# Two attention layers on one core: the last half block of the first layer turned on TensorE, and two sets of first scores placed anew

## The chip, the cores and the metric

The kernel runs on one core of a Trainium2 chip. Its time is the device time of one execution in microseconds, the median of several runs; the profile is of one execution of the same program. Five engines take part, each with its own instruction queue: TensorE (PE, with its weight loads PEld), VectorE (DVE), ScalarE (ACT), GpSimd (POOL) and SyncE (SP). DMAs are issued here from SP and POOL. Each queue runs in order: an instruction that waits holds up all that stand behind it on its engine.

## The reference

Two attention layers on an image batch x of shape 4 x 64 x 64 x 256, that is 4 images of N = 4096 tokens with C = 256 channels, in fp32.

```python
# layer 0
q, k, v = x @ Wq + bq, x @ Wk + bk, x @ Wv + bv          # 32, 32, 256 channels
attn = softmax(einsum('bnd,bmd->bnm', q, k))
x1 = gamma * einsum('bnm,bmc->bnc', attn, v) + x
# layer 1
f, g, v = x1 @ Wf + bf, x1 @ Wg + bg, x1 @ Wh + bh        # 32, 32, 128 channels
beta = softmax(einsum('bqd,bkd->bqk', g, f))
out = x1 + (einsum('bqk,bkd->bqd', beta, v) @ Wo + bo)
```

Layer 1 of an image needs the whole of layer 0 of that image: its keys and values come from every token of x1.

## The kernel before, in words

**Steps.** For each image b and layer l the queries are worked off in blocks j, and for each block all keys in steps i. Layer 0 has 16 blocks of 256 queries with 8 steps of 512 keys; layer 1 has 8 blocks of 512 queries with 16 steps of 256 keys. That is 128 steps a layer and 1024 in all, numbered n. In a step TensorE makes the scores (keys by queries, `Step.scores`, L595) into PSUM, ACT takes their exponential p (L611), and TensorE multiplies p by the values into an accumulator (L655 in layer 0, L673 in layer 1).

**Exact products in parts.** Where a step is split, p is cut into a high part (a second exponential on ACT, L605), a low part (DVE, L625) and a correction d (DVE, L630), and so are the values; TensorE then makes three sets of faster products, called "h", "l" and "d". All steps of layer 0 are split, and the even steps of layer 1; the odd steps of layer 1 take p whole. DVE also adds up the p of layer 1 for the softmax's denominator (p_sum, L644); some p are added by DMA instead (p_sum_moved, issued by POOL, L618 and L620). The p of these steps keep their SBUF buffer until that DMA has landed.

**PSUM.** Eight banks: the tag "st" holds one set of scores (two banks), "pair" two banks, which in layer 0 are the accumulators of the second half of the queries and in layer 1 a second buffer for scores, "acc0" and "acc1" one bank each, and "side" two buffers of one bank for everything else. In layer 1 the scores alternate between "st" and "pair"; in layer 0 all scores use "st", the first of each image too. The scores of step n + 2 are issued in step n.

**Projections between the steps.** While a step runs, small stages are put at given places: `put(n, slot, ...)` hangs a stage on step n, at "a" (before the step's cuts) or at "b" (after the scores of step n + 2). `plan` hangs them, at the first step of each block, by strings such as "2b 5a 5b": step offset and slot. A half block of 256 tokens goes through the stages load, turn (transposed to channels by tokens, xT), cut and rest (xT in a high and a low part, xh and xl), five stages for queries and keys (multiply into psqk, L439; take; add; cut; rest, which stores the result to qk_dram, L469), and three for the values (multiply into psv, L490; take; rest). The keys of both half blocks of 512 tokens are then loaded from qk_dram by four DMAs that POOL issues (L529), as soon as both are stored.

**How a half block is turned.** Only the 16 half blocks of image 0 in layer 0 are transposed by TensorE: natural tiles x_nat and an identity into a side bank, and ACT copies that to xT (L400, L401). All others are read from DRAM in 32 x 32 squares by eight DMAs (`load_squares`, L287), and DVE transposes inside the squares (L403). For layer 1 they are squares of x1_dram, which the end of each layer 0 block stores.

**The end of a layer 0 block.** `end_first` adds the accumulator halves (o, L693) and puts `residual(0)` and `residual(1)`, one for each 128 queries: x_new = o times gamma over the sum, plus x, on DVE (L701, L702, L704), a store to x1_dram on SP (L708), and an accumulating DMA to the output on POOL (L709). For all blocks but the last they hang on steps 1 and 2 of the next block; for the last on steps 0 and 1 of layer 1.

**The last half block.** Block 15 of layer 0 ends where layer 1 begins. Its half block, h = 15, is planned at the first step of layer 1 (`put_half(n, b, NH - 1, ...)`), with its load in step 2, its turn in step 5 and its projection in step 7. The keys of block 7, of which it is half, are used first by the scores of step 14, which are issued in step 12. In the same block the half block 15 of the next image is loaded (offset 9) and turned on DVE (offset 11).

**Order.** From step 8 on the order of instructions is the order in which the program writes them (`manual_schedule`); each engine's queue is that order. In a layer 1 step it is: stages of slot "a"; the cuts on DVE; the scores of step n + 2; stages of slot "b"; the sums that are due; the products "h" and "l" or the whole ones of this step; the "d" of the step before.

**Buffers that matter.** "small" has four buffers of 128 x 256 (x_res, x_new, y), "sums" one of 128 x 512 (the folded p_sum of a layer 1 block, idle in most of layer 0), "squares" two (squares, xh, xl and reloaded xT in turn).

Of the kernel before, what the change touches and what calls it, by code (L numbers as in the profile page):

```python
# [50 lines left out]
F32 = mybir.dt.float32  # L51
# [6 lines left out]
P = 128  # L58
QB = 512
# [188 lines left out]
def fast_path(ctx: ExitStack, tc: tile.TileContext, x, w0, w1, wo, bo, gamma, out, off):  # L248
# [46 lines left out]
            load_squares((b, 0, h), x[b, h * QB0 : (h + 1) * QB0, :])  # L295


    x_nat = {}
    LEAD_BUFS = sum(split[1])
    LEAD = V1 // NS  # L300

    def load_first(h):
        if h < NH:
            x_nat[h] = []
            for n in range(h * NS, (h + 1) * NS):
                x_nat[h].append(data.tile([P, C], F32, tag="v1", bufs=V1, name=f"x_nat_{n}"))
                nc.sync.dma_start(x_nat[h][-1], x[0, n * P : (n + 1) * P, :])

    for h in range(LEAD):
        load_first(h)  # L310


    ident = work.tile([P, NT, QB0], F32, tag="moved", bufs=1, name="ident")[:, 0, :P]
    make_identity(nc, ident)
    ones = const.tile([P, 1], F32, name="ones")
    nc.vector.memset(ones, 1.0)

# [31 lines left out]
    def side_psum(name):  # L349
        return ps_side.tile([P, QB], F32, tag="side", name=name)  # L350
# [38 lines left out]
    def transpose_stages(b, l, h):  # L389
        key = (b, l, h)  # L390
        lead = b == l == 0 and h % 2 == 1

        def turn():
            tag = "v1_parts" if lead else "xT"
            xT[key] = data.tile([P, NCC, QB0], F32, tag=tag, bufs=LEAD_BUFS if lead else 1, name=f"xT_{b}_{l}_{h}")
            if b == l == 0:
                ps = side_psum(f"psx_{h}").rearrange("p (c n) -> p c n", c=NCC)
                for c in range(NCC):
                    for t in range(NS):
                        nc.tensor.transpose(ps[:, c, t * P : (t + 1) * P], x_nat[h][t][:, c * P : (c + 1) * P], ident)  # L400
                nc.scalar.copy(xT[key], ps)  # L401
            else:
                nc.vector.transpose(  # L403
                    xT[key].rearrange("p c n -> p (c n)"), turned[key].rearrange("p c n -> p (c n)")
                )

        def cut():
            x_parts[key] = [
                (data if lead else work).tile(
                    [P, NCC, QB0],  # L410
                    F32R,
                    tag="v1_parts" if lead else "squares",
                    bufs=LEAD_BUFS if lead else 2,
                    name=f"x{what}_{b}_{l}_{h}",
                )
                for what in "hl"
            ]
            nc.scalar.copy(x_parts[key][0], xT[key])

        def rest():  # L420
            nc.vector.tensor_sub(x_parts[key][1], xT[key], x_parts[key][0].bitcast(F32))
            if b == l == 0:
                load_first(h + LEAD)

        return turn, cut, rest
# [149 lines left out]
    class Step:  # L575
# [10 lines left out]
        def scores(self):  # L586
            b, l, j, i = self.b, self.l, self.j, self.i
            n = 2 * QB // G[l]
            q0 = j * n % QB
            index = j * NI[1] + i  # L590
            tag = "pair" if l == 1 and index > 0 and index % 2 == 0 else "st"
            st = ps_main.tile([P, G[l], n], F32, tag=tag, name=f"st_{self.key}")
            for g in range(G[l]):
                kt = G[l] * i + g
                nc.tensor.matmul(  # L595
                    st[:, g, :],
                    k_t[b, l, kt // NT][:, kt % NT * P : (kt % NT + 1) * P],
                    q_t[b, l, j * n // QB][:, q0 : q0 + n],
                    start=True,
                    stop=True,  # L600
                )
            s_flat = st.rearrange("p g n -> p (g n)").rearrange("p (a n) -> p a n", n=QB0)
            if self.split:
                self.high = wide(f"high_{self.key}", self.n + 0.6, F32R)
                nc.scalar.activation(self.high, s_flat, AF.Exp, bias=down)  # L605
            kept = self.n - 0.3 if l == 0 else self.n + 1.8
            if l == 1 and i in self.moved:
                moved_until[0] = max(moved_until[0], self.n - 0.4) + 2.3
                kept = max(kept, moved_until[0])
            self.p = wide(f"p_{self.key}", kept)  # L610
            nc.scalar.activation(self.p, s_flat, AF.Exp)  # L611
# [77 lines left out]
    def end_first(b, j, acc, o, n_next):  # L689

        key = f"{b}_{j}"
        for s in range(NS):
            nc.vector.tensor_add(o[s], o[s], acc[2 * s + 1][:, :W])  # L693
        jj, part = divmod(j, QB // QB0)
        x_old = x_res.pop((b, j))

        def residual(s):
            def issue():
                n = (b * N + j * QB0) // P + s
                g = work.tile([P, 1], F32, tag="g", name=f"g_{key}_{s}")  # L700
                nc.vector.reciprocal(inverse[:, 0, n : n + 1], o[s][:, C : C + 1])  # L701
                nc.vector.tensor_mul(g, inverse[:, 0, n : n + 1], gamma_sb)  # L702
                x_new = small(f"x1_{key}_{s}")
                nc.vector.scalar_tensor_tensor(x_new, o[s][:, :C], g, x_old[s], ALU.mult, ALU.add)  # L704
                if part == 0 and s == 0:
                    x1_dram[b, jj] = dram.tile([QB, C], F32, name=f"x1_dram_{b}_{jj}")
                row = part * QB0 + s * P
                nc.sync.dma_start(x1_dram[b, jj][row : row + P, :], x_new)  # L708
                nc.gpsimd.dma_start(out_rows(b, j, s), x_new, accum_op=ALU.add)  # L709

            return issue

        n_next += j < NQ[0] - 1
        put(n_next, "b", residual(0))
        put(n_next + 1, "b", residual(1))

    def take_first_two(b, j, acc):

# [79 lines left out]

    def put_half(n, b, h, at):
        (turn, cut, rest), qk, v = project_stages(b, 1, h)  # L800
        load = lambda: load_squares((b, 1, h), x1_rows(b, h))
        put_all(n, at, (load, turn, cut, rest, qk[0], qk[1], qk[2], qk[3], qk[4], v[0], v[1], v[2]))

    def put_next(n, b, h, at):
# [10 lines left out]
    def put_values(m, b, h):  # L815
# [8 lines left out]
        put(m + 1, "a", v[1])  # L824
        put(m + 1, "b", v[2])

    def plan(n, b, l, j):
        if l == 0 and j >= 1:
            put_half(n, b, j - 1, "3b 5b 5b 6b 7b 8a 8b 8b 9b 8b 9a 11b")
            if b + 1 < B:  # L830
                put_next(n, b + 1, j - 1, "0b 1b 1b 2b 3b 4a 4b 4b 5b")
        if l == 1:
            if j == 0:
                put_half(n, b, NH - 1, "2b 5a 5b 6a 7b 8a 8b 8b 9a 8b 9a 9b")
            if b + 1 < B:
                if j == 0:
                    put_next(n, b + 1, NH - 1, "9b 11a 11b 12a 13b 14a 14b 14b 15b")
                else:
                    first, at = VALUES_AT[j]
                    for k, m in enumerate(at):  # L840
                        put_values(n + m, b + 1, first + k)
# [41 lines left out]
    for n, s in enumerate(steps):  # L883
# [50 lines left out]
        if l == 1:  # L934
            if s.last:
                o = take_first_two(b, j, acc)
            later.scores()
            run(todo.pop((n, "b"), []))

            while later_sums and (later_sums[0][1] <= n or vector_clock + later_sums[0][0] <= tensor_clock + AHEAD_OF):  # L940
                took, _, issue, _ = later_sums.pop(0)
                issue()
                vector_clock += took
            behind = steps[n - 1] if not s.first and steps[n - 1].split else None
            if s.last and behind:
                behind.products_second(acc, ("d",))
            s.products_second(acc, ("h", "l") if s.split else ("whole",))
            if not s.last and behind:
                behind.products_second(acc, ("d",))
            if s.last:  # L950
                vector_clock += 0.8
                end_second(b, j, acc, p_sum, o, n + 1)
        else:

            for half, what in ((0, "h"), (0, "l"), (1, "h"), (1, "l")) if s.first or s.last else ((0, "h"), (1, "h"), (0, "l"), (1, "l")):
                s.products_first(acc, half, what)
                if s.last and what == "l":
                    take_first(b, j, acc, o, half)
            if early:
                run([u for x in early for u in x[1] + x[2]])  # L960
            later.scores()
            run(todo.pop((n, "b"), []))
            for half in (0, 1):
                s.products_first(acc, half, "d")
            if s.last:
                end_first(b, j, acc, o, n + 1)
# [65 lines left out]
```

## Time and profile before

| | |
|---|---|
| Median of 3 runs | 3156.79 us (3154.54 to 3158.68) |
| Profiled execution, its own time | 3157.77 us |
| Its span, first to last instruction | 3155.9 us |
| Granted TensorE clock over the span | 0.995 |
| Instructions | 55119 |
| Steady layer 0, 100 to 515 us | PE busy 415.00 us, DVE 374.87, ACT 291.86 |
| First block of layer 1, image 0, 526 to 575 us | PE busy 43.88 of 49.00 us, DVE 42.05, ACT 32.90; clock 0.97 |
| Rest of layer 1, image 0, 575 to 830 us | PE busy 254.68 of 255.00 us, DVE 227.98, ACT 184.99 |

Rows of the groups view give for each kind of instruction its count and the mean time of one. Those that the change touches:

| Instruction | Count | Mean ns |
|---|---|---|
| transpose on TensorE, psx (L400) | 64 | 273 (median), pipelined |
| copy of it by ACT (L401) | 16 | 577 |
| transpose in squares on DVE (L403) | 112 | 708 |
| low and d cuts on DVE (L625, L630) | 534 and 527 under their first names | 1222, 1220 |
| x_new on DVE (L704) | 128 | 485 |
| store of x1 on SP, to landing (L708) | 128 | 1.7 us |
| square load from x1 on SP, to landing (L287) | 512 | 1.9 us |

A line of the timeline reads: start in us, length of the merged row, engine, source line, operation, what is written and read, how many instructions, and in brackets the engine's idle time before it and who ended that. PE rows are pipelined: the start of one row to the start of the next is the time that the engine gave to it. Idle time of DVE, ACT or POOL costs nothing by itself.

### The profile page before, as it was taken

To read this page: it belongs to the slowest core of one execution; us is meant where nothing else is said; L and a number is where in the kernel's file an instruction comes from. 1 tells how busy PE (TensorE), PEld (TensorE's weight loads), DVE (VectorE), ACT (ScalarE), POOL (GpSimd) and SP (SyncE) were. 2 spreads that over 40 slices of the span, in tenths; PEclk is the share of its full clock that TensorE was granted. 3 is DMA by queue.
4 is the path that set the end of the run, shared out by engine and by line. 5 is a ranking of instruction groups with operands and counts; after the bars stand their busy time and mean duration, and the time that the engine had idled before them with its cause. 6 is when DMAs were issued, how large, how long until landed. Compare 5 with 4: busy or idle time off the path is not lost. (4 is left out here: it accounts for less than half of the span.)

```text
span 3155.9 us, 55119 instructions
## 1 busy us (share of the span) xinstructions
PE 3099.8 (98%) x20036; PEld 2696.1 (85%) x20036; DVE 2755.2 (87%) x3360; ACT 2203.1 (70%) x2899; POOL 773.2 (24%) x1137
## 2 busy tenths in 40 slices
PE   8999999999999999999999999999999999999998
PEld 7999998666799999766679999976668999996665
DVE  7899889888888899898889998988887888888897
ACT  7677777677667677677766777767776666667775
POOL 4111113222411111322241111132234111132322
PEclk9999999999999999999999999999999999999999
DMA  4344445556644444656554444465565333335655
GB/s 123 75 93 85 90 88 122 121 115 121 121 84 89 87 93 84 131 117 118 118 107 93 84 92 84 94 129 114 118 123 99 65 65 73 63 82 113 116 107 94
DMA packets 446746, 314.55 MB, mean 100 GB/s; under 512 B 272802, under 2 KB 394404, under 8 KB 446468
## 3 DMA queue, kind: packets, MB, share of 16 engines
q0 software_dynamic: 109392, 184.43, 32.8%
q1 hardware_dynamic: 336164, 126.19, 16.9%
q8 instruction: 162, 2.65, 0.3%
q14 instruction: 116, 0.95, 0.1%
q10 hardware_dynamic: 912, 0.33, 0.0%
HBM read 128.71 MB, written 96.47 MB: 71 GB/s over the span
## 5 line engine op out<-in xcount | busy, mean ns | idle before, releaser
L605 ACT ACTIVATE high<-st,down 128x1024 fp32r<-128x1024 f32 x645 | 721.0, 1118 | 696.1 <-PE st L595 605.2
L611 ACT ACTIVATE p<-st 128x1024 f32<-128x1024 f32 x1024 | 1026.5, 1019 | 17.2 <-DMA p_sum_moved<-p 9.7
L625 DVE TENSOR_TENSOR low<-p,high 128x1024 fp32r<-128x1024 f32 x534 | 652.7, 1222 | 123.8 <-ACT p L611 119.4
L595 PE MATMUL st<-q,k 128*128 128x256 f32 (+1 forms) x3072 | 663.4, 324 | 13.3 <-DMA k<-qk_dram 7.4
L630 DVE SCALAR_TENSOR_TENSOR d<-low,high 128x1024 fp32r<-128x1024 f32 x527 | 643.0, 1220 | 15.6 <-PE acc L673 0.7
L595 PEld LDWEIGHTS st<-q,k 128*128 128x128 f32 x3072 | 473.4, 189 | 73.4 <-issue 16.4
L673 PE MATMUL acc<-p,v 128*128 128x512 f32 x1024 | 488.8, 600 | 1.1 <-DVE o L744 1.1
L655 PE MATMUL acc<-v0d,d 128*128 128x258 f32 x2048 | 336.1, 286 | 2.1 <-DVE d L630 2.0
L655 PE MATMUL acc<-v0h,high 128*128 128x258 f32 x2048 | 330.9, 284 | 1.2 <-ACT high L605 1.2
L655 PE MATMUL acc_pair<-v0l,low 128*128 128x256 f32 (+1 forms) x2048 | 329.9, 283 | 0.0
L655 PE MATMUL acc_pair<-v0h,high 128*128 128x258 f32 x2048 | 329.7, 283 | 0.0
L655 PE MATMUL acc_pair<-v0d,d 128*128 128x258 f32 x2048 | 328.8, 282 | 0.0
L655 PE MATMUL acc<-v0l,low 128*128 128x256 f32 (+1 forms) x2048 | 328.0, 282 | 0.6 <-DVE low L625 0.5
L709 POOL DMA_DIRECT2D out<-x x128 | 114.4, 894 | 837.0 <-DVE x L704 828.9
L644 DVE TENSOR_TENSOR p_sum<-p_sum,p 128x1024 f32<-128x1024 f32 x257 | 313.0, 1218 | 0.3
L673 PEld LDWEIGHTS acc<-p,v 128*128 128x128 f32 x1024 | 188.4, 191 | 144.2 <-issue 123.6
L655 PEld LDWEIGHTS acc<-v0d,d 128*128 128x128 f32 x2048 | 281.0, 189 | 3.8 <-DVE d L630 3.7
L655 PEld LDWEIGHTS acc<-v0h,high 128*128 128x128 f32 x2048 | 281.5, 189 | 3.0 <-issue 1.4
L655 PEld LDWEIGHTS acc<-v0l,low 128*128 128x128 f32 x2048 | 280.9, 189 | 1.8 <-DVE low L625 1.6
L655 PEld LDWEIGHTS acc_pair<-v0l,low 128*128 128x128 f32 x2048 | 282.3, 189 | 0.1
L655 PEld LDWEIGHTS acc_pair<-v0h,high 128*128 128x128 f32 x2048 | 281.9, 189 | 0.2 <-DVE o L693 0.2
L655 PEld LDWEIGHTS acc_pair<-v0d,d 128*128 128x128 f32 x2048 | 281.6, 189 | 0.0
(157 smaller groups left out, 4281.6 us busy)
## 6 DMA issues: line engine op xcount, KB each, us to landing
p_sum_moved<-p POOLq DMA_DIRECT2D x191, 512.0 KB, 4.8
x_res<-in_x SPq DMA_DIRECT2D x128, 128.0 KB, 3.1
qk_dram<-qk_parts SPq DMA_DIRECT2D x128, 128.0 KB, 2.1
x_res<-bias POOLq DMA_DIRECT2D x128, 128.0 KB, 4.0
out<-bias SPq DMA_DIRECT2D x128, 128.0 KB, 4.2
x_dram<-x SPq DMA_DIRECT2D x128, 128.0 KB, 1.7
out<-x POOLq DMA_DIRECT2D x128, 128.0 KB, 3.1
squares<-x_dram SPq DMA_DIRECT2D x512, 32.0 KB, 1.9
```

What stands on the lines that cost most here:

```text
L595: nc.tensor.matmul(st[:, g, :], k_t[b, l, kt // NT][:, kt % NT * P : (kt % NT + 1) * P], q_t[b, l, j * n // QB][:, q0 : q0 + n], start=Tru ...
L605: nc.scalar.activation(self.high, s_flat, AF.Exp, bias=down)
L611: nc.scalar.activation(self.p, s_flat, AF.Exp)
L625: nc.vector.tensor_sub(self.low, self.p, self.high.bitcast(F32))
L630: nc.vector.scalar_tensor_tensor(self.d, self.low.bitcast(F32), -UP, self.high.bitcast(F32), ALU.mult, ALU.add)
L644: nc.vector.tensor_add(p_sum, other, self.p)
L655: nc.tensor.matmul(acc[2 * s + which][:, :width], p[:, g, s * P : (s + 1) * P], v0[self.i][v][:, g, :width], start=self.first and what != ...
L673: nc.tensor.matmul(acc[which], v_part[:, g, :], p[:, g * NS : (g + 1) * NS, :], start=first and g == 0, stop=last and g == G[1] - 1,)
L709: nc.gpsimd.dma_start(out_rows(b, j, s), x_new, accum_op=ALU.add)
```

## The change

The x_new tiles of block 15 stay in SBUF and are transposed by TensorE into a side bank with an identity; ACT copies the bank to xT. They are not stored to x1_dram any more, and their half block isn't loaded in squares. The identity is written to DRAM once at the start, and each image loads it at block 8 of layer 0 into the "sums" buffer, since the SBUF place where it was made is reused. The residual of block 15 is hung on step 0 of layer 1, its first part at "a". The stages of the last half block move up: turn from offset 5 to 3, projection from 7 to 5. The first scores of layer 0 of images 1 to 3 use "pair" in place of "st". In the first step of layer 1 the products "h" and "l" come ahead of the scores of step 2.

```diff
-    x_nat = {}
+    rows = {}
...
+            rows[0, 0, h] = (tiles, ident)
...
     make_identity(nc, ident)
+    ident_dram = dram.tile([P, P], F32, name="ident_dram")
+    nc.sync.dma_start(ident_dram, ident)
...
-            if b == l == 0:
-                ps = side_psum(f"psx_{h}").rearrange("p (c n) -> p c n", c=NCC)
+            if key in rows:
+                tiles, unit = rows.pop(key)
+                ps = side_psum(f"psx_{b}_{l}_{h}").rearrange("p (c n) -> p c n", c=NCC)
                 for c in range(NCC):
                     for t in range(NS):
-                        nc.tensor.transpose(ps[:, c, t * P : (t + 1) * P], x_nat[h][t][:, c * P : (c + 1) * P], ident)
+                        nc.tensor.transpose(ps[:, c, t * P : (t + 1) * P], tiles[t][:, c * P : (c + 1) * P], unit)
                 nc.scalar.copy(xT[key], ps)
...
-            tag = "pair" if l == 1 and index > 0 and index % 2 == 0 else "st"
+            in_pair = index > 0 and index % 2 == 0 if l == 1 else b > 0 and j == i == 0
+            tag = "pair" if in_pair else "st"
...
                 x_new = small(f"x1_{key}_{s}")
+                if j == NQ[0] - 1:
+                    if s == 0:
+                        rows[b, 1, NH - 1] = ([], idents.pop(b))
+                    rows[b, 1, NH - 1][0].append(x_new)
...
-                nc.sync.dma_start(x1_dram[b, jj][row : row + P, :], x_new)
+                if j < NQ[0] - 1:
+                    nc.sync.dma_start(x1_dram[b, jj][row : row + P, :], x_new)
...
-        n_next += j < NQ[0] - 1
-        put(n_next, "b", residual(0))
-        put(n_next + 1, "b", residual(1))
+        if j < NQ[0] - 1:
+            put(n_next + 1, "b", residual(0))
+            put(n_next + 2, "b", residual(1))
+        else:
+            put(n_next, "a", residual(0))
+            put(n_next, "b", residual(1))
...
-        load = lambda: load_squares((b, 1, h), x1_rows(b, h))
+        load = nothing if h == NH - 1 else lambda: load_squares((b, 1, h), x1_rows(b, h))
...
+    def load_ident(b):
+        idents[b] = work.tile([P, QB], F32, tag="sums", bufs=1, name=f"ident_{b}")[:, :P]
+        nc.sync.dma_start(idents[b], ident_dram)
...
+        if l == 0 and j == NQ[0] // 2:
+            put(n, "b", lambda: load_ident(b))
...
-                put_half(n, b, NH - 1, "2b 5a 5b 6a 7b 8a 8b 8b 9a 8b 9a 9b")
+                put_half(n, b, NH - 1, "2b 3a 3b 4a 5b 6a 6b 6b 7a 7b 8a 8b")
...
+            if s.first and j == 0:
+                s.products_second(acc, ("h", "l"))
             later.scores()
...
-            s.products_second(acc, ("h", "l") if s.split else ("whole",))
+            if not (s.first and j == 0):
+                s.products_second(acc, ("h", "l") if s.split else ("whole",))
```

More of the change, by code (lines that the diff above doesn't have):

```diff
@@ L303, in load_first @@
         if h < NH:
-            x_nat[h] = []
+            tiles = []
             for n in range(h * NS, (h + 1) * NS):
-                x_nat[h].append(data.tile([P, C], F32, tag="v1", bufs=V1, name=f"x_nat_{n}"))
-                nc.sync.dma_start(x_nat[h][-1], x[0, n * P : (n + 1) * P, :])
+                tiles.append(data.tile([P, C], F32, tag="v1", bufs=V1, name=f"x_nat_{n}"))
+                nc.sync.dma_start(tiles[-1], x[0, n * P : (n + 1) * P, :])
+            rows[0, 0, h] = (tiles, ident)
+    ident = work.tile([P, NT, QB0], F32, tag="moved", bufs=1, name="ident")[:, 0, :P]
     for h in range(LEAD):
         load_first(h)
-    ident = work.tile([P, NT, QB0], F32, tag="moved", bufs=1, name="ident")[:, 0, :P]
     make_identity(nc, ident)
+    ident_dram = dram.tile([P, P], F32, name="ident_dram")
+    nc.sync.dma_start(ident_dram, ident)
     ones = const.tile([P, 1], F32, name="ones")
@@ L825, in put_values @@
         put(m + 1, "b", v[2])
+    idents = {}
+    def load_ident(b):
+        idents[b] = work.tile([P, QB], F32, tag="sums", bufs=1, name=f"ident_{b}")[:, :P]
+        nc.sync.dma_start(idents[b], ident_dram)
     def plan(n, b, l, j):
+        if l == 0 and j == NQ[0] // 2:
+            put(n, "b", lambda: load_ident(b))
         if l == 0 and j >= 1:
```

## The prediction

> **What bounds the kernel now.** I read the page's engine line first, then the waits of TensorE (PE), then the timeline around the places that these waits name, then the queues of the engines that end them.
>
> ```profile
> PE 3099.8 (98%) x20036; PEld 2696.1 (85%) x20036; DVE 2755.2 (87%) x3360; ACT 2203.1 (70%) x2899; POOL 773.2 (24%) x1137
> ```
> TensorE is the bound, with 56 us idle in 3155.9 us. Only its idle time, or matmuls that run slowly, can be won, unless work is taken from it; the change adds some. The waits of PE say where:
>
> ```profile
> PE st L595 <- DMA k<-qk_dram: 7.4, 4, 3.0
> PE acc L673 <- DVE v0l L625: 4.0, 2, 3.6
> PE st L595 <- ACT p L611: 3.6, 3, 1.2
> PE st L595 <- DVE o L693: 2.3, 4, 0.6
> ```
> Columns: total, times, longest. They come 4, 2, 3 and 4 times: once per image or at an image's end, and not in the steady blocks (PE is busy 415.00 of 415.00 us from 100 to 515). The places are the first block of layer 1 in each image (526-575, 1302-1352, 2081-2130, 2852-2905 us) and the three changes of image (841, 1619, 2399 us).
>
> The wait for k, in image 2, and what follows it:
> ```profile
> 2112.94 1.19 PE L595 MATMUL st<-q,k 128*128 128x512 f32 x2 [2.99 <-DMA k<-qk_dram]
> 2113.93 1.05 PE L673 MATMUL acc<-high,v 128*128 128x512 f32 x2
> 2114.78 1.05 PE L673 MATMUL acc<-v0h,v 128*128 128x512 f32 x2
> ```
> The next matmul pairs start 0.85 us apart. The same pairs elsewhere start 0.47 apart (838.66, 839.13, 839.60 below): after such a wait PE runs at about half rate for some 3 us, so the wait costs more than its idle time.
>
> Why k is late: the chain of the last half block (x1 stored, reloaded in squares, transposed on DVE) stands on DVE like this in image 1:
> ```profile
> 1310.63 4.38 SPq L287 DMA_DIRECT2D squares<-x_dram  x8
> 1319.19 0.71 DVE L403 STREAM_TRANSPOSE xT<-squares 128x512 f32<-128x512 f32 x1 [2.84 <-DMA squares<-x_dram]
> 1319.83 1.18 DVE L625 TENSOR_TENSOR v0l<-p,high 128x1024 fp32r<-128x1024 f32 x1
> ```
> DVE stops 2.84 us for the squares; the low part of step 6 queues behind, and PE waits 3.55 us for it (1.0, 0.6, 0.6 in the other images). The change of image:
> ```profile
> 838.66 0.63 PE L595 MATMUL st<-q,k 128*128 128x256 f32 x4
> 839.13 0.63 PE L673 MATMUL acc<-high,v 128*128 128x512 f32 x2
> 839.60 0.62 PE L673 MATMUL acc<-low,v 128*128 128x512 f32 x2
> 841.41 0.74 PE L595 MATMUL st<-q,k 128*128 128x256 f32 x4 [1.19 <-ACT p L611]
> ```
> The second scores of the new image want the st buffer that the first ones still hold until their exponentials are through.
>
> **The Trainium skill.** TensorE: Matmul & The Clock Gate, section What's actually happening: the array's clock has two states, half and full, and falls to half after an idle window of about 3.4 us. The trace agrees on the factor (0.85 against 0.47), but shows the fall after waits of 2.6-3.6 us and not after 1.2. VectorE: DVE Perf Modes, section The three transpose paths: DVE transposes only 32x32 blocks, TensorE a full 128x128 into PSUM; here the former needs eight square loads per half block, the latter a copy out of PSUM by ACT. The trace has both paths (L403; L400 with L401). DMA: Bandwidth & Descriptors, section Latency and other measured facts: a DMA through HBM has about 2 us of fixed cost; here x_dram lands after 1.7 and squares after 1.9 us at the median, two in series.
>
> **The change, part by part.** I count a stretch of PE per image, from the last acc_pair product of layer 0 to the first whole product of layer 1's second block: starts 526.43 to 571.48 = 45.05 us, 1302.34 to 1348.92 = 46.58, 2081.30 to 2125.67 = 44.37, 2852.44 to 2892.61 = 40.17. Comparing start-to-start times with the undisturbed ones (0.235 per 512-wide product, 0.43 per half of a plain fp32 one, 0.11 per 256-wide one), lost time is:
> - scores of step 2 waiting for DVE's o: 0.84 each image;
> - low of step 6: 1.27, 5.36, 0.90, 0.88, slow matmuls included;
> - k: 5.08, 2.15, 4.74, 1.33, included likewise;
> - DVE's o or d at the block's end: 0.77, 1.13, 0.77, 0.49.
> Sums 7.96, 9.48, 7.25, 3.54. What is left is 37.1 in images 0-2 and 36.6 in image 3, which has no projection of a next image: the accounts close.
>
> Removed: two stores of x1, eight square loads (4 us of SP's issue) and one DVE transpose (0.71) per image. The stores and loads leave SP, which is not on PE's path except through these waits. Added on PE: four transposes per image, 0.11 apart at full clock (the four from 21.06 take 0.60, of which 0.27 is the length of the last), 4 x 0.11 = 0.45, in all 1.8 us, fully on the bound. Added on ACT: one PSUM copy of 0.57 between the exponentials of steps 4 and 5; ACT was idle 1.19 us after them, which hides it. Added on SP: one 64 KB load of the identity per image, half an image ahead, and one store at the start behind the first eight x_nat loads: nothing.
>
> Scores of step 2 behind the h and l products of step 0: DVE's o is done at 527.24, those products (4 x 0.235) run to 527.5, so this 0.84 goes. The scores come 0.2 later on ACT, which is within slack.
>
> k: transposes now stand before step 3's scores, projection in step 5. On DVE the last qk piece (L466) ends at about 545.4 instead of 550.16, SP stores it, 2 to 3.4 us to landing, four k loads on POOL take 2.0 and 2.3 to land: k is there at 551.5-553.5. PE wants it at about 554.5. The k wait with its slow clock goes, all of 13.3 us. On SP the next image's squares follow that store, so DVE's 3.91 us stop for them at 557.73 shrinks too. Without k before it POOL would move p of step 9 earlier; now it is behind k and lands near 556. Its buffer's next user wants it at 557 (p of step 15 in images 2 and 3) or later: nothing, with 1 us in hand.
>
> What is late next is DVE. From 526.33 to 571.33 it was idle 5.93 us; 45.0 - 5.93 - 0.71 = 38.4 us of work, against 37.1 + 0.45 = 37.55 for PE. Walking its queue with these durations, the residual's six instructions now come before the low of step 2 (done 532.0, wanted 532.45), low of step 4 is 0.1-0.2 late, low of step 6 ends at 542.15 where PE comes at 541.5. At the block's end DVE's o still follows p of the new block by 6.0 us from its scores, PE wants it 5.5 us after: 0.7 stays. So DVE's 38.4 plus some 0.9 of waiting for ACT gives 39.3 in images 0-2: gains 5.8, 7.3, 5.1. Image 3: 3.54 - 0.45 - 0.8 (low of step 6) - 0.4 = 1.9. Together 20.1 us.
>
> Changes of image: with the first scores in the pair buffer, 1.34 per change is freed on PE (1.19 idle and the restart), 4.0 in all. Behind them DVE's d of the first step is due about 0.4 early for DVE in images 0 and 2: gain 0.9 each. In image 1 DVE waits there for a moved sum until 1624.99 (0.95) and PE already waits 0.66 for the d after it: that DMA does not come earlier, gain 0. Sum 1.8; bounds 0 and 4.0.
>
> Total 21.9 us. The profiled execution took 3157.77 (span 3155.9 and 1.9 around it), so 3135.9; the median of the runs shown is 0.98 lower, so 3135.
>
> **Rivals.** A, above. B: the residual DVE waits vanish as well: PE's floor, 26.4 in the stretches after 1.8 for the transposes, and 4.0 at the image changes, 30.4: 3126. For it: DVE has 10% idle in layer 1. Against: 38.4 is more than 37.55. C: DVE stays late by more: the new projection waits for the side PSUM slot, which DVE frees at 537.6 with PE there at 537.9, or the next image's squares still stop DVE for 2.5 us in three images, and the image changes give nothing: 21.9 - 7.5 - 1.8 = 12.6, 3144. D, slower: POOL now holds the moved sum of step 9 behind four k loads that wait for a store. If that store lands late, p of step 15 or the next block's exponential waits for the buffer, ACT stops and PE with it. This decides from 1 us of lateness on, and to lose it must eat 22/4 = 5.5 us per image; at 7.5 us per image over the gain-free 3157 it gives 3165. The k store's 3.4 us at the worst so far speaks against. E, no effect: every freed wait forms again on DVE; it would need 22 us of DVE work that the rows do not show; 3156.
>
> **Chances.** A 0.65, B 0.12, C 0.17, D 0.03, E 0.03. Faster or slower means by over 0.2% (6.3 us), about what a measurement of this kernel can tell from no change: faster is A, B and C, 0.94; same E, 0.03; slower D, 0.03. The range reaches from B's time to C's and one more: 3126 to 3145.
>
> **What will show it.** No wait of PE's scores on k, and none on p at the image changes; matmul pairs at 0.47 throughout 526-575; no squares<-x_dram in step 3 of layer 1; four psx transposes 0.11 apart; a remaining wait of 0.6-0.9 us for a low of step 6, and 0.5-0.7 for o at the block's end in images 0 and 2. Wrong it would be if PE waits for psqk's slot, if ACT shows a wait on p_sum_moved in the first block, or if the stretch stays above 41 us.

## The result and the profile after

| | Before | After |
|---|---|---|
| Median | 3156.56 us, 6 runs (3154.12 to 3159.48) | 3136.31 us, 6 runs (3134.36 to 3137.30) |
| Ratio | | 0.9935, 95% interval 0.9922 to 0.9947 |
| Profiled execution, its span | 3157.77, 3155.9 us | 3135.21, 3133.3 us |
| Stretches of images 0 to 3 | 45.05, 46.58, 44.37, 40.17 | 38.74, 38.77, 38.81, 38.03 |
| Changes of image | 37.17, 38.22, 37.14 | 36.60, 37.10, 36.98 |

The stretch is that of the prediction. A change of image is counted from the last but seventh whole product of layer 1 to the 96th acc_pair product of the next image. The stretches gained 6.31, 7.81, 5.56 and 2.14, together 21.8 us; the changes of image 1.85; the rest of layer 1 in image 2 lost 1.1 (its end waits 2.78 us for v0d in place of 1.94, at a place that the change doesn't touch). That is the 22.6 us between the spans, as the smaller differences elsewhere, 0.5 us at most, cancel. The medians are 20.25 apart: the profiled execution of before lies 1.2 us above its median, that of after 1.1 below.

The engine line of the page of after, and its waits of PE (total, times, longest):

```profile
PE 3095.0 (99%) x20052; PEld 2694.6 (86%) x20052; DVE 2752.9 (88%) x3356; ACT 2204.0 (70%) x2903; POOL 773.5 (25%) x1137
```

```profile
PE acc L660 <- DVE d L635: 3.9, 8, 0.6
...
PE pso L767 <- DVE v0d L523: 3.2, 3, 2.8
...
PE psqk L443 <- DVE xl L425: 0.8, 4, 0.2
PE acc L678 <- DVE o L757: 0.7, 3, 0.3
...
PE st L600 <- ACT p L616: 0.4, 1, 0.4
```

PE did 16 instructions more, the transposes, and was busy 4.8 us less, though the work grew. Fewer matmuls ran at half rate: between 200 and 3100 us the granted clock drops to half for 3.41 us four times in the trace of before (from 559.84, 1321.01, 2112.90 and 2385.97) and once in that of after (from 2366.12, at the end of layer 1 of image 2). Of the old list the wait for k from qk_dram (7.4 us) and those for the low cuts of L625 in layer 1 (4.0 us under the name v0l, 1.6 each under v0h and v0d) are gone, that for p fell from 3.6 to 0.4. The d that layer 0 waits for (L660) now stands first, and a wait of 0.2 per image for xl is new.

The scores that had waited 2.99 us for k in image 2, those of step 14, in the timeline of after (second line):

```profile
2092.10 1.03 PE L678 MATMUL acc<-v0d,v 128*128 128x512 f32 x2
2092.97 0.63 PE L600 MATMUL st<-q,k 128*128 128x512 f32 x2
2093.43 0.62 PE L678 MATMUL acc<-high,v 128*128 128x512 f32 x2
2093.89 0.62 PE L678 MATMUL acc<-v0h,v 128*128 128x512 f32 x2
```

They have no brackets, so no wait, and the pairs start 0.46 apart: the full clock. By stage: in the windows 526-575, 1302-1352 and 2081-2130 us the granted clock was 0.97 each before and is 1.00 each after.

DVE in image 1, in after:

```profile
1320.04 1.22 DVE L649 TENSOR_TENSOR p_sum<-p_sum,p 128x1024 f32<-128x1024 f32 x1
1321.18 0.70 DVE L407 STREAM_TRANSPOSE xT<-squares 128x512 f32<-128x512 f32 x1
1321.81 1.18 DVE L630 TENSOR_TENSOR v0d<-p,high 128x1024 fp32r<-128x1024 f32 x1
```

The transpose for which DVE had stopped 2.84 us in image 1 is gone. The one shown is the only one left in the stretch, that of the next image's half block, and it comes without a stop: its squares had landed 1.5 us earlier here, and 0.8 us earlier in images 0 and 2.

The change to image 1, on PE in after:

```profile
837.70 0.64 PE L600 MATMUL st<-q,k 128*128 128x256 f32 x4
838.76 0.73 PE L660 MATMUL acc<-v0d,d 128*128 128x258 f32 x4 [0.42 <-DVE d L635]
839.32 0.66 PE L660 MATMUL acc_pair<-v0d,d 128*128 128x258 f32 x4
```

The scores wait for nothing, and 1 us later the products wait for d. What is left in the stretch shows in step 5:

```profile
537.42 0.28 PE L443 MATMUL psqk<-xh,wqk 128*128 128x256 f32 x1
537.90 0.39 PE L443 MATMUL psqk<-xl,wqk 128*128 128x256 f32 x1 [0.20 <-DVE xl L425]
538.13 0.28 PE L443 MATMUL psqk<-xh,wqk 128*128 128x256 f32 x1
```

The first two start 0.48 apart and the next 0.23, against 0.12 each when nothing is missing: 0.2 of idle costs 0.47 from start to start. With 0.3 for a d and 0.4 for o at the block's end that makes up the 1.2 us per image (1.0 in image 3) over PE's floor, which is 37.55 (37.05 in image 3) by the forecast's account.

### The profile page after: what moved, and what is told of

Same layout as the page of the kernel before. It is cut to its first block, busy times and chain, and to the rows that moved or that the text cites. A ratio compares the mean times of both kernels' runs of the same rounds, so it can differ in the third digit from the quotient of the medians.

```text
span 3133.3 us, 55070 instructions
## 1 busy us (share of the span) xinstructions
PE 3095.0 (99%) x20052; PEld 2694.6 (86%) x20052; DVE 2752.9 (88%) x3356; ACT 2204.0 (70%) x2903; POOL 773.5 (25%) x1137
## 4 chain that ended last, share of the span: by engine, by line
PE 89%; DVE 4%; issue 2%; DMA 2%; ACT 1%; POOL 1%; SPq 0%; POOLq 0%; ACTq 0%; DVEq 0%
PE acc L660 23%; PE acc_pair L660 23%; PE acc L678 21%; PE st L600 14%; PE psv L494 4%; PE psqk L443 2%; DMA p_sum_moved<-p 2%; PE pso L767 2%; POOL k L533 1%; ACT p L616 1%; DVE p_sum L649 1%; PE pso L768 0%; DVE v0d L630 0%; DVE v0h L635 0%; DVE d L635 0%
## 5 line engine op out<-in xcount | busy, mean ns | idle before, releaser
L660 PE MATMUL acc<-v0d,d 128*128 128x258 f32 x2048 | 336.6, 286 | 4.1 <-DVE d L635 3.9
L660 PE MATMUL acc<-v0h,high 128*128 128x258 f32 x2048 | 331.0, 284 | 1.2 <-ACT high L610 1.2
L660 PE MATMUL acc_pair<-v0l,low 128*128 128x256 f32 (+1 forms) x2048 | 330.0, 283 | 0.0
L660 PE MATMUL acc_pair<-v0h,high 128*128 128x258 f32 x2048 | 329.6, 283 | 0.0
L660 PE MATMUL acc_pair<-v0d,d 128*128 128x258 f32 x2048 | 328.8, 282 | 0.0
L660 PE MATMUL acc<-v0l,low 128*128 128x256 f32 (+1 forms) x2048 | 327.9, 282 | 0.6 <-DVE low L630 0.5
L660 PEld LDWEIGHTS acc<-v0d,d 128*128 128x128 f32 x2048 | 281.0, 189 | 6.9 <-DVE d L635 5.0
L660 PEld LDWEIGHTS acc<-v0h,high 128*128 128x128 f32 x2048 | 281.5, 189 | 3.0 <-ACT high L610 1.4
L660 PEld LDWEIGHTS acc_pair<-v0l,low 128*128 128x128 f32 x2048 | 282.3, 189 | 0.1
L660 PEld LDWEIGHTS acc<-v0l,low 128*128 128x128 f32 x2048 | 280.9, 189 | 1.6 <-DVE low L630 1.6
L660 PEld LDWEIGHTS acc_pair<-v0h,high 128*128 128x128 f32 x2048 | 281.9, 189 | 0.0
L660 PEld LDWEIGHTS acc_pair<-v0d,d 128*128 128x128 f32 x2048 | 281.6, 189 | 0.0
```

Source lines behind the costliest of these rows:

```text
L660: nc.tensor.matmul(acc[2 * s + which][:, :width], p[:, g, s * P : (s + 1) * P], v0[self.i][v][:, g, :width], start=self.first and what != ...
```

## The experiments

All but pair_only start from the changed kernel; each ratio is to the kernel before, measured beside it. Theory 1 at the outset: the gain is k in time, and what bounds the stretch then is the amount of DVE's work. Its second half fell.

**late_stages: the new path, the stages where they stood.**

```diff
-put_half(n, b, NH - 1, "2b 3a 3b 4a 5b 6a 6b 6b 7a 7b 8a 8b")
+put_half(n, b, NH - 1, "2b 5a 5b 6a 7b 8a 8b 8b 9a 8b 9a 9b")
```

> The changed kernel with the last half block's stages at their old places (turn in step 5 of layer 1, projection in step 7); the transposes stay on TensorE. Theory 1 (the gain is k's lateness, and k comes in time because the stages stand earlier): the scores of step 14 wait for k again, 2 to 3 us in images 0 to 2 and about 1 in image 3, with slow matmuls behind; the stretch (last acc_pair product of layer 0 to the first whole product of layer 1's second block) is 42 to 43.5 us in images 0 to 2, about 40 in image 3; median near 3149. Rival 2 (the gain is the path itself: no store, no reload, no transpose on VectorE): no such wait, stretches below 39.5, median at most 3139.

3148.92 us (9 runs), ratio 0.9974 [0.9964, 0.9984]; stretches 42.98, 43.31, 43.17, 39.39. The timeline of PE in image 1:

```profile
1334.45 0.69 PE L600 MATMUL st<-q,k 128*128 128x512 f32 x2 [2.06 <-DMA k<-qk_dram]
1334.98 0.61 PE L678 MATMUL acc<-high,v 128*128 128x512 f32 x2
1336.19 1.22 PE L678 MATMUL acc<-v0d,v 128*128 128x512 f32 x2 [0.59 <-DVE v0d L630]
1337.21 1.05 PE L600 MATMUL st<-q,k 128*128 128x512 f32 x2
```

k is late again in every image (1.60, 2.06, 1.74, 1.18 us), with a wait for the low cut behind it and pairs 1.02 and 0.85 apart in images 0 to 2. Of 21.8 us in the stretches the rest of the change (the new path, the order of the first step, the earlier residual) brings 7.3, moving the stages up 14.5. k's lateness comes from when the stages stand: shown.

**squares_early: the old path, with the stages moved up.** x1 of block 15 is stored and read back in squares, with no identity.

```diff
-load = nothing if h == NH - 1 else lambda: load_squares((b, 1, h), x1_rows(b, h))
+load = lambda: load_squares((b, 1, h), x1_rows(b, h))
...
-put_half(n, b, NH - 1, "2b 3a 3b 4a 5b 6a 6b 6b 7a 7b 8a 8b")
+put_half(n, b, NH - 1, "1b 4a 4b 5a 6a 6b 7a 7a 7b 7b 8a 8b")
```

> The changed kernel with x1 of block 15 stored and reloaded in squares as before, but with the load one step earlier (step 1), turn on VectorE in step 4 and projection in step 6. Theory 1: k is in time, no wait of the scores for it; VectorE stops 1 to 2 us for the squares and has 0.7 more work, so that the stretch is 40 to 41 us in all of images 0 to 2; median 3141 to 3145. Rival 2: near the kernel before, 3150 or more.

3147.57 us, 16 runs that spread from 3141.18 to 3156.31; ratio 0.9973 [0.9965, 0.9982]. The longer of them had the lower mean granted clock (0.998 in the shortest, 0.994 in the two longest), so they spent more time at half rate. The profiled execution took 3143.66, near the short end. Its stretches are 41.54, 41.50, 40.91, 39.57. No wait for k; DVE and PE in image 0:

```profile
539.24 0.71 DVE L407 STREAM_TRANSPOSE xT<-squares 128x512 f32<-128x512 f32 x1 [1.57 <-DMA squares<-x_dram]
```

```profile
541.11 0.73 PE L678 MATMUL acc<-d,v 128*128 128x512 f32 x2 [1.38 <-DVE d L635]
542.84 0.39 PE L443 MATMUL psqk<-xl,wqk 128*128 128x256 f32 x1 [0.89 <-DVE xl L425]
```

DVE's stop for the squares comes out on PE, as waits for what queues behind it on DVE. In these stretches 12.6 of the 21.8 us are won with the old path. The other 9.2 come with turning on TensorE, which also lets turn, cut and multiply stand half a step to a step earlier than here. By the medians the two parts are 9.3 us (to the kernel before) and 11.3 (to the changed one), as the profile is of a short execution.

**pair_only: the kernel before, with the first scores of images 1 to 3 in the pair buffer.**

```diff
-tag = "pair" if l == 1 and index > 0 and index % 2 == 0 else "st"
+in_pair = index > 0 and index % 2 == 0 if l == 1 else b > 0 and j == i == 0
+tag = "pair" if in_pair else "st"
```

> The kernel before with only the first scores of images 1 to 3 in the pair buffer. Theory 1: the wait of the second scores for p (1.19 three times) goes, but VectorE's d takes back half: 1.8 us faster, median near 3154.8, and waits of a first d of 0.4 to 0.6 appear at the changes of image. Rival: all of 4.0 us is won, 3152.6.

3156.05 us (12 runs), ratio 0.9998 [0.9989, 1.0007]; changes of image 36.74, 38.03, 36.99: gains of 0.43, 0.19, 0.15. The wait of the scores for p is gone, and behind it:

```profile
844.61 0.64 PE L596 MATMUL st<-q,k 128*128 128x256 f32 x4
845.67 0.72 PE L656 MATMUL acc<-v0d,d 128*128 128x258 f32 x4 [0.43 <-DVE d L631]
```

Most of the freed 1.34 us forms again on DVE's cuts, in two or three waits of 0.26 to 0.65 per change.

**no_pair: the changed kernel without it.**

```diff
-in_pair = index > 0 and index % 2 == 0 if l == 1 else b > 0 and j == i == 0
+in_pair = index > 0 and index % 2 == 0 and l == 1
```

> The changed kernel with the first scores of images 1 to 3 back in st. Theory 1 (the image changes gained 0.57, 1.12 and 0.16 from the pair buffer, and the stretches have nothing to do with it): changes back to 37.2, 38.2 and 37.1, stretches as in the changed kernel, about 2 us slower, 3138. Rival (as when the pair buffer was put into the kernel before alone: DVE is late by nearly as much, gains of 0.43, 0.19 and 0.15): changes of 37.0, 37.3 and 37.1, less than 1 us slower, 3136.5 to 3137.

3135.57 us (5 runs), ratio 0.9932 [0.9918, 0.9945], no slower than the changed kernel. Its waits of PE:

```profile
PE st L600 <- ACT p L616: 3.6, 3, 1.2
...
PE acc L660 <- DVE d L635: 2.0, 4, 0.6
```

Without the pair buffer PE waits 3.2 us more for p and 1.9 less for d. The changes of image sum to 112.0 here. In runs that all have the pair buffer and don't touch this place the sum goes from 110.6 (qk_later) and 110.7 (after) over 111.8 (drop_sum) and 112.4 (drop_early) to 112.7 (scores_first). The 1.85 us that I read from one pair of profiles is no more than this scatter: the placement shows no effect on the time, and both theories asked for more than was there.

**scores_first: the scores of step 2 back ahead of the products of step 0.**

```diff
-if s.first and j == 0:
-    s.products_second(acc, ("h", "l"))
 later.scores()
...
-if not (s.first and j == 0):
-    s.products_second(acc, ("h", "l") if s.split else ("whole",))
+s.products_second(acc, ("h", "l") if s.split else ("whole",))
```

> The changed kernel with the scores of layer 1's step 2 ahead of the products h and l of step 0 again. Theory 1 as in the prediction (0.84 us of TensorE's own time per image): the wait for VectorE's o returns and stretches grow by 0.8, median near 3139.6. Rival (VectorE's work of 38.4 us bounds the stretch, so that an earlier wait of TensorE hides in it): the wait returns, but stretches grow by at most 0.3, median within 3136 to 3137.5.

3135.40 us (4 runs), ratio 0.9934 [0.9917, 0.9951]. The timeline of PE has the wait back, in all images:

```profile
526.86 0.73 PE L600 MATMUL st<-q,k 128*128 128x512 f32 x2 [0.59 <-DVE o L698]
```

But the stretches grew only by 0.34, 0.25, 0.21 and 0.32, since the wait for xl (0.47 us) is gone where this one (0.84) comes. In the time it doesn't show.

**residual_late and copy_on_dve: DVE's work ahead of xl later, and more of it.**

```diff
-put(n_next, "a", residual(0))
-put(n_next, "b", residual(1))
+put(n_next, "b", residual(0))
+put(n_next + 1, "b", residual(1))
```

> The changed kernel with the residual of block 15 at its old places (end of step 0 and of step 1 of layer 1). Theory 1 (x_new is ready 3 us before the transposes want it, and the order on VectorE matters little): stretches within 0.3 us of the changed kernel's 38.7 to 38.8, median 3135.5 to 3137.5. Rival (the earlier residual is what lets the transposes come in time): TensorE waits for x in its psx transposes and the stretch grows by over 0.6 us, median 3139 or more.

3137.19 us (4 runs), ratio 0.9944 [0.9927, 0.9960]; stretches 39.23, 39.25, 39.29, 38.51, so 0.48 to 0.49 more each, between the two forecasts. The transposes wait for nothing, against the rival; PE waits 0.32 to 0.34 for the low of step 4 instead. In the block behind the stretch PE waits 0.95 to 1.0 for p in three images.

```diff
-nc.scalar.copy(xT[key], ps)
+(nc.vector.tensor_copy if l == 1 else nc.scalar.copy)(xT[key], ps)
```

> The changed kernel with the copy of the transposed half block out of PSUM on VectorE in place of ScalarE (layer 1 only). If VectorE bounds the stretch (its queue has no idle time there): stretches grow by the copy, 0.5 to 0.7 us, median near 3138.7. If TensorE bounds it: at most 0.2, median 3136 to 3137.

3138.46 us (4 runs), ratio 0.9946 [0.9930, 0.9963]; stretches 39.33, 39.38, 39.40, 38.63. The copy starts 0.61 ahead of the low of step 4 (535.63 and 536.24), and PE:

```profile
537.51 0.73 PE L678 MATMUL acc<-v0d,v 128*128 128x512 f32 x2 [0.57 <-DVE v0d L630]
...
538.91 0.38 PE L443 MATMUL psqk<-xl,wqk 128*128 128x256 f32 x1
```

The stretches grow by 0.59 to 0.61, all that the copy delays the cut: there is no slack on DVE at this place. I took that for proof that DVE's amount bounds the stretch. It isn't, as drop_sum shows.

**qk_later: the projection half a step to a step later.**

```diff
-put_half(n, b, NH - 1, "2b 3a 3b 4a 5b 6a 6b 6b 7a 7b 8a 8b")
+put_half(n, b, NH - 1, "2b 3a 3b 4a 6a 6b 7a 7a 7b 7b 8a 8b")
```

> The changed kernel with the multiply and the following stages of queries and keys half a step later, so that TensorE does not wait for xl (0.37 and 0.12 us of slow restart per image now). If TensorE bounds the stretch: 0.3 to 0.5 us less per image, stretches near 38.3, median near 3134.7. If VectorE bounds it: the wait moves to another place of TensorE, stretches stay at 38.6 to 38.8, median 3135.5 to 3137.

3138.43 us (4 runs), ratio 0.9945 [0.9928, 0.9961]; stretches 39.22, 39.74, 39.33, 38.01. The wait for xl is gone, but the stretches of images 0 to 2 grew, which neither forecast had: PE waits elsewhere, in image 0 for a d inside the stretch and for p behind its end:

```profile
561.68 0.73 PE L678 MATMUL acc<-v0d,v 128*128 128x512 f32 x2 [0.57 <-DVE v0d L635]
571.21 0.73 PE L600 MATMUL st<-q,k 128*128 128x512 f32 x2 [1.35 <-ACT p L616]
```

**next_later: the next image's half block out of this block.** Its stages go to the second block of layer 1.

```diff
-put_next(n, b + 1, NH - 1, "9b 11a 11b 12a 13b 14a 14b 14b 15b")
+put_next(n + NI[1], b + 1, NH - 1, "10b 12a 12b 13a 15b 16a 16b 16b 17b")
```

> The changed kernel with the projection of the next image's last half block moved out of layer 1's first block into its second one. This takes about 2.3 us of VectorE's work and 0.45 of TensorE's out of the stretch. If VectorE bounds the stretch: stretches of images 0 to 2 fall to about 37.3 (TensorE's floor), 0.45 comes back in the second block, median near 3133. If TensorE bounds it: stretches fall by 0.45, which comes back later, median 3136.

3139.42 us (4 runs), ratio 0.9952 [0.9936, 0.9969]; stretches 38.05, 38.09, 38.10, 38.05, the length of image 3, which has no next image. They fell by 0.7, between the two forecasts. It is lost again in the second block, where reloads of xT now stand on SP behind the store of q and k (606.22 in image 0, three reloads from 606.65 on):

```profile
PE psv L494 <- DMA xT_again<-xT_dram: 5.1, 3, 1.8
```

**drop_sum and drop_early: one addition of DVE less, behind xl or ahead of it.** They leave the p of step 4, or of step 2, out of the denominators of block 0.

```diff
-if self.l == 0 or self.i in self.moved:
+if self.l == 0 or self.i in self.moved or (self.j == 0 and self.i == 4):
```

> The changed kernel, but DVE leaves out one of its additions to p_sum (step 4 of block 0 of layer 1, one per image, 1.22 us of DVE), so one step is missing in that block's softmax denominators. Theory 1 (in the changed kernel the stretch is as long as DVE's work of 38.4 to 38.7 us; PE's own floor there is 37.55, and 37.05 in image 3): the stretches fall from 38.74, 38.77, 38.81, 38.03 to 37.6 to 37.8 and 37.1 to 37.3, the waits of psqk for xl and of acc for d at the block's end nearly vanish, about 4 us in all, 3132. Rival (PE's rest of waits hangs on where single instructions stand in DVE's order, not on the amount of DVE's work): the stretches fall by less than 0.4 each, 3135 to 3136.

3136.02 us (5 runs), ratio 0.9935 [0.9922, 0.9949]; stretches 38.75, 38.79, 38.80, 38.05: nothing. 1.22 us of DVE is gone, and DVE turned most of it into stops, in its timeline:

```profile
544.82 0.42 DVE L470 TENSOR_TENSOR qk_parts<-qk_parts 64x256 fp32r<-64x256 f32 x1 [0.47 <-ACT qk_parts L466]
...
549.30 1.23 DVE L630 TENSOR_TENSOR low<-p,v0d 128x1024 fp32r<-128x1024 f32 x1 [0.42 <-ACT p L616]
...
561.90 1.23 DVE L630 TENSOR_TENSOR v0h<-p,high 128x1024 fp32r<-128x1024 f32 x1 [0.18 <-ACT p L616]
```

The last of these, which after has too (0.18 at 560.79), stands ahead of o, so the block's end waits as before; and xl stands ahead of the missing addition. Theory 1 falls, its rival holds. The same edit with step 2, whose addition stands ahead of xl:

> The changed kernel, but DVE leaves out the addition of step 2 in block 0 of layer 1 (one per image, 1.22 us of DVE ahead of xl), so one step is missing in that block's softmax denominators. After leaving out the addition of step 4, which stands behind xl, changed no stretch, theory 2: only DVE's work ahead of xl sets what PE still loses in step 5 (0.2 idle and a restart, about 0.45 to 0.5), and the loss at the block's end hangs on the exponential of the last steps, not on DVE's amount. Expected: xl's wait goes, stretches of 38.2 to 38.4 and 37.5 to 37.7, some 1.8 us less in the span, too little for the times to show. Rival (theory 1, total work, or PE is at its floor): no change of the stretches, 38.75 and 38.05, although the wait for xl goes.

3133.32 us (5 runs), ratio 0.9926 [0.9913, 0.9940], an interval that overlaps that of the changed kernel; stretches 38.20, 38.20, 38.20, 37.52. The first two psqk start 0.12 apart, without a wait:

```profile
537.02 0.28 PE L443 MATMUL psqk<-xh,wqk 128*128 128x256 f32 x1
537.14 0.28 PE L443 MATMUL psqk<-xl,wqk 128*128 128x256 f32 x1
```

The stretches fell by 0.51 to 0.61, a little more than the 0.47 read for the wait for xl. The same 1.22 us of DVE is worth some 0.55 us ahead of xl and nothing behind it.

**moved_more: that addition given to a DMA.**

```diff
 self.moved = MOVED_LAST if b == B - 1 and j == NQ[1] - 1 else MOVED_SUMS
+if l == 1 and j == 0:
+    self.moved = (1,) + MOVED_SUMS
```

> The changed kernel, but in block 0 of layer 1 the p of step 1 is added by DMA as well (seven moved steps in place of six), so DVE does one addition of 1.22 us less in the stretch, with all of the computation kept. Theory 1: if the chain of moved sums has room on POOL, the stretches fall as without one addition, to 37.6 to 37.8 and 37.1 to 37.3, 3132. Rival (POOL and the buffers are next: each moved sum takes 3 to 5 us to land and the next one waits for it on POOL, ahead of the loads of k, while p keeps its buffer): ACT's exponentials wait for p_sum_moved or PE's scores for k, the stretches stay at 38.5 or grow, 3136 to 3145.

3139.43 us (5 runs), ratio 0.9945 [0.9931, 0.9959]; stretches 39.82, 40.01, 40.13, 38.05. The wait for xl goes here too, but then, on DVE and PE of image 0:

```profile
553.79 0.71 DVE L407 STREAM_TRANSPOSE xT<-squares 128x512 f32<-128x512 f32 x1 [1.85 <-DMA squares<-in_x]
```

```profile
555.67 0.74 PE L680 MATMUL acc<-v0l,v 128*128 128x512 f32 x2 [0.97 <-DVE v0l L632]
...
561.95 0.73 PE L680 MATMUL acc<-v0d,v 128*128 128x512 f32 x2 [0.56 <-DVE v0d L637]
```

Counted from the start of the stretch, the issue of the next image's squares began at 18.2 us in place of 19.3, but took 4.98 us in place of 3.87, and the last landed at 27.1 in place of 25.3 (image 0). Inside the stretches of images 0 to 2 PE waits neither for k nor for p, which the rival had expected: its range was right, its mechanism was not, and the price is paid by the squares. Whether the additional DMA slowed their issue was not tried. Image 3 has no such squares and gains nothing either; PE waits 0.69 for q there.

None of these is measurably quicker than the changed kernel with all of its computation kept; scores_first and no_pair equal it.

## Why the prediction was right

The time (3136.31, forecast 3135), the sum of the stretches (21.8, forecast 20.1) and the likeliest course, A, came out. Its core, k in time through earlier stages, is shown by late_stages. That the sum came so near is in part luck: terms that were too small and too large cancel. By its steps:

- **k.** Right, the largest term: no scores wait for k. Image 0, whose stretch begins 0.51 earlier than before (525.92 against 526.43): DVE's last piece ended at 544.81 (forecast 545.4), SP's store left at 544.84, and k landed at 549.62 to 551.00, a little ahead of 551.5-553.5, as the store landed in 1.7 us where 2 to 3.4 was taken. The wait and the slow matmuls went, and late_stages brought both back; it puts 14.5 us on the earlier places, what waits behind k included, where 13.3 was forecast for k alone.
- **Low of step 6.** I let 0.8 per image stay; nothing did. The cut ended at 541.25, which is 541.76 in the forecast's times and so 0.4 ahead of 542.15, and PE came for it at 541.48, 0.5 behind its forecast time, as it had lost 0.47 at xl. The 0.4 is a fault of my walk of DVE's queue: it added up the durations of the rows, but neighbours overlap. From 525.82 on the 22 rows up to this cut sum to 15.85 us in the trace of after and took 15.43. The term, 0.8 in four images, is larger than the 1.7 us by which the sum of the stretches was forecast too low; xl's wait, below, took part of it back.
- **Scores of step 2.** The wait of 0.84 went as said, but is not worth 0.84: scores_first shows 0.2 to 0.35, for the same time is waited for at xl instead. The term was too large, and xl's wait, 0.47, was not in the forecast; my walk of DVE's queue named only the low cuts and left out the stage's own cut.
- **Block's end.** o was to wait 0.5 to 0.7 in images 0 and 2: idle 0.23 and about 0.4 with the restart, in images 0 to 2. Right in place.
- **"What is late next is DVE", 38.4 us of work plus 0.9.** The number was near, the reason only half. The 38.4 counts some 0.7 of short gaps between instructions as work: in after DVE is busy 37.66 us in the 38.74 of image 0's stretch. DVE's amount doesn't set the stretch (drop_sum). What does is PE's floor and two places where one DVE instruction comes late: xl, after all that stands ahead of it (drop_early shows it), and the block's end, where DVE's cut follows ACT's p (read from the timelines; no run moved it, so this part is not shown). copy_on_dve and residual_late alone would have kept the wrong reason alive.
- **Transposes.** 4 x 0.11 was right: in image 0 they take 0.35 to the next start (532.38 to 532.73), and the scores behind them 0.1 more than their 0.46.
- **Changes of image.** 1.8 was forecast and 1.85 read, but by accident: 0.9, 0, 0.9 against 0.57, 1.12, 0.16. Image 1 gained the most where I had set nothing, and no_pair has 37.13 there without the pair buffer. The length of this change goes with the landing of a moved sum: DVE waits 1.54 to 1.74 us for it in the runs with the pair buffer where the change took 38.0 to 38.2 (pair_only and drop_early among them) and 0.6 to 0.7 where it took 37.0 to 37.2 (after, drop_sum); in no_pair it doesn't wait for it. In images 0 and 2 the first d is 0.42 to 0.45 late, as forecast; what was left out is a second one in the step behind, 0.13 and 0.53 late. The placement's true worth is within the scatter.
- **Rivals.** B falls, as 1.0 to 1.3 us per image is left over the floor. C's mechanism, a stop for the next image's squares, didn't come, but they landed only 0.8 us ahead of their transpose in images 0 and 2, and in moved_more the stop is there. D falls: the moved sum of step 9 had landed at 554.34, and nothing waited for it on PE's path. E falls with the first row of the result.

## What to carry to other kernels

When a late transfer starves the bounding engine, follow its chain back to what sets its start. Here an earlier place ended the wait for k with the old path too (squares_early), and the shorter path took away the stop of DVE that an earlier place brings with it. How the gain is split between the two depends on which is taken away: 14.5 us are lost without the earlier places, some 9 to 11 without turning on TensorE, at places a little later. Before an engine's amount of work is called a bound, take some away at two places, ahead of and behind the instruction that is waited for: adding work shows only that the place is tight. And a wait that is removed counts only for what the next wait behind it doesn't take back; for 1 us or two that has to be read from several profiles, not from one pair.

## What the runs showed of the hardware

- Half rate came after shorter idle times than the 2.6 us of the forecast: in late_stages after 1.60 and, 1.2 us later, another 0.55 us of idle (image 0; likewise 2.06 and 0.59, 1.74 and 0.61), and already in the trace of before after 1.94 at the end of layer 1 of image 2 (half rate from 2385.97). After 1.18 alone (image 3 of late_stages) pairs stayed 0.47 apart; so did they after 0.71 and 0.96 in image 1 of before.
- The traces show a pattern behind this. The granted clock is at half in pieces of 3.41 us, and the starts of these pieces lie whole multiples of 3.413 us apart (223, 232 and 80 of them in before; 227 and 227 in late_stages), on a fixed grid. From 200 us to 40 us before the end the 14 traces hold 15 such drops. In the grid piece just ahead of each, PE was idle for 1.73 us or more, about half of it; behind pieces with less there was no drop, behind pieces with more than 1.8 always, and between 1.73 and 1.78 both occurred. So two short waits in one piece count together, and the price of a wait depends on how it falls on the grid. The Trainium skill (TensorE: Matmul & The Clock Gate, What's actually happening) speaks of one idle window of about 3.4 us; the length agrees, but here a window that was idle for half its time was enough.
- A short idle time cost PE more than itself: 0.20 us of waiting for xl cost 0.47 us, which came back in full when the wait went (0.51 to 0.61 in drop_early).
- DVE instructions of 1.22 us overlapped where the second doesn't need the first: in drop_sum 1.13 from the start of d at 538.88 to the low cut at 540.01, but 1.33 from that cut to the d that reads it. This queue, walked with durations alone, comes out late: 0.42 us over 22 rows.
